# Weights in three tiles, another order of the projections, and where biases and key differences are computed, in an attention and expert kernel

## The chip, the cores and the metric

The kernel runs on one core of a Trainium2 chip. The metric is the device time of one execution in microseconds. Before the change three runs gave 4274.84, 4279.24 and 4280.67, median 4279.24. The profile is of another execution, which took 4282.12.

## The reference

The input x has 4 sequences of 2048 tokens with 512 features, in float32. It is normalized (layer norm), and two things are added to x: self-attention with 16 heads of 32 features, whose queries and keys pass a spectral filter, and a top-1 choice among 8 experts with 100 places each, which all share one weight.

```python
xn = _layernorm(x, axis=-1)
# attention
qkv = xn @ w_qkv
q, k, v = jnp.split(qkv, 3, axis=-1)          # then (B, H, S, dh)
mask = jax.nn.sigmoid(mask_logits)
q = _spectral_filter(q, mask)                 # rfft over dh, times mask, irfft
k = _spectral_filter(k, mask)
scores = jnp.einsum('bhqd,bhkd->bhqk', q, k) / math.sqrt(dh)
attn = jax.nn.softmax(scores, axis=-1)
out = jnp.einsum('bhqk,bhkd->bhqd', attn, v)
out = out.transpose(0, 2, 1, 3).reshape(B, S, D) @ w_out + b_out
# experts: each token's best one, the first 100 tokens of each
expert_out = dispatched @ w_expert + b_expert
combined = combine.reshape(-1, E * C) @ expert_out
x = x + out + combined
```

## The kernel before, in words

**Groups, blocks, halves.** The work is cut into 16 groups k: batch b = k // 4 and four heads c = k % 4. A group has four blocks n of 512 queries, a block 16 halves, one for each tile j of 128 keys, so a group has 64 halves (`GH`) and a block 16 (`HB`). Two halves, an even and an odd j, form a window. The whole main loop (lines 1013 to 1066) has 1024 halves. Every tensor is float32.

**What a half does.** For the heads in two pairs u: TensorE computes two products for the row maxima of a later block (`max_matmuls`, lines 497 to 507), 20 halves ahead of their use, and the two score tiles of this block (`scores`). The scores have keys in the partitions and go to banks 0 to 3 of the array. They are not computed from keys but from `steps_of_keys`, the difference of a key tile from the tile before it (`key_steps`, line 442), and added to what the bank holds; a block starts by writing the negated maxima there (`shift`). ScalarE takes exponentials of both (128x1024 each), VectorE reduces the products of the maxima (`max_reduce`, line 509), and TensorE multiplies the probabilities of the half before with the values (`products`, line 670), whose sum VectorE forms in `num`. Then come the half's planned steps, from `agenda`.

**Banks.** Banks 4 to 7 rotate (`turns`) among the maxima (two a pair), the products (one) and every planned step that uses TensorE (one). A maximum is one reduction for two neighbouring banks where u is 0 in the stream and the two are neighbours; else two.

**Row sums.** The row sums are formed by adding all probability tiles of a block: an accumulating DMA that GpSimd issues adds the odd tile to the even one (`pair`, 1 MB), and GpSimd adds the even tile of the window before (`add_to`), two instructions of 128x1024.

**Maxima of a block.** When all maxima of a block exist, VectorE takes the negated maximum (`max_negate`), TensorE transposes it at the next even half (`max_close`, line 527), ScalarE copies it to `row` and `rest`, GpSimd splits it at the start of the next window into three bfloat16 parts (`max_split`), and SP's queue moves the three rows to `negm`, which `shift` reads at the start of the block.

**Planned steps.** `plan` (line 907) lays into the halves of group k what the group k + 1 needs. Each of its 48 pieces (`projections`, line 469) is 16 matmuls over one tile of 128 tokens, for a query, a key or a value. `spread` (line 846) walks through the pieces in their order and finds the lowest level at which all fit before the half `last`; each half's `costs` count what is planned there already. Keys may come only after the old keys are spent (`after_keys_are_spent`, the bound `SPENT`), and the key differences come at 54, 58, 62 and 66 halves after the group's start. The list of groups `CROWDED` has another order. The weights of a group are one tile `wg` of three parts (query, key, value) with one buffer, loaded again (`load_qkv_weights`, line 414) after the last piece that reads it.

**Closing a block.** `close_steps` (line 689): row sums to `den` at half 5 of the next block, eight reciprocals on VectorE at halves 6 to 13, the division on GpSimd, four output projections at halves 17 to 20 (`result`, line 707: TensorE, then ScalarE copies the bank into `y`), then an accumulating DMA from `y` to the output.

**The token stage.** In the third group of a batch (c = 2) the next batch is loaded tile by tile (`load_tile`), measured on VectorE (`bn_stats`, `bn_aggr`), given the attention's output bias on GpSimd (`bias`, line 251) and written to the output (`first_sums`, line 255), onto which the later DMAs accumulate. In the fourth group the tiles are loaded again, normalized on ScalarE and turned on TensorE (`turn`) into `xnT`. For the first batch the load, the bias and the write stand in group 0.

**What sets the order.** Each engine runs its instructions in the order of the program (`InOrder`); SP's queue issues its DMAs in the same way. Line 84 is the helper that records every operation, so the profile's groups are told apart by tiles.

Of the kernel before, what the change touches and what calls it, by code (L numbers as in the profile page):

```python
# [25 lines left out]
P = 128  # L26
# [77 lines left out]
def attention_and_top1_experts(ctx: ExitStack, tc: tile.TileContext, a: dict, out: bass.AP):  # L104
# [90 lines left out]
    def filter_steps(c):  # L195
# [13 lines left out]
        def filtered(s):  # L209
# [6 lines left out]
            if c == 0:  # L216
                on.scalar.copy(wg[0][:, :, s, :], done)
            else:
                on.scalar.copy(wt[:, 1, :], pw)
                nc.sync.dma_start(out=wd[c][:, :, s, :], in_=wt[:, 1, :].rearrange("p (r n) -> p r n", r=NR))  # L220
# [9 lines left out]
    def token_stage(b):  # L230
# [20 lines left out]
        def bias(i):  # L251
            row = held[i // TQ][:, i % TQ, :]
            on.gpsimd.tensor_tensor(row, row, b_out, ALU.add)

        def first_sums(i):

            n, t = divmod(i, TQ)
            on.sync.dma_start(out=o[b, n, :, t : t + 1, :], in_=held[n][:, t : t + 1, :])
# [149 lines left out]
        return load, measure, scale, normalize, turn, route, bias, first_sums, load_tile  # L408
# [5 lines left out]
    def load_qkv_weights(k):  # L414
        wg[k] = weights.tile([P, NR, 3, P], F32, name="wg", bufs=1)
        on.sync.dma_start(out=wg[k], in_=wd[k % NG])
# [12 lines left out]
    def query_key(k, n, s, first, last):  # L429
# [3 lines left out]
        for r in range(NR):  # L433
            columns(pq, wg[k][:, r, s, :], xnT[:, r, cols], start=(r == 0), stop=(r == NR - 1))
# [7 lines left out]
    def key_steps(n):  # L442

        here = slice(n * QB, (n + 1) * QB)
        on.gpsimd.tensor_tensor(
# [6 lines left out]
    def value(k, n, first, last):  # L452
# [3 lines left out]
        for t in range(first, last):  # L456
            i = n * TQ + t
            for r in range(NR):
# [3 lines left out]
                    wg[k][:, r, 2, :],  # L462
# [6 lines left out]
    def projections(k, tiles=1):  # L469
# [5 lines left out]
        else:  # L475
            late = [(value, n) for n in range(2, NQ)] + [(query_key, 1, 0)]
            order = [(query_key, 0, 0)] + [(value, n) for n in range(2)] + (late if k not in CROWDED else [])
            order += [(query_key, n, 1) for n in range(NQ)] + (late[::-1] if k in CROWDED else [])
            order += [(query_key, n, 0) for n in range(2, NQ)]
# [29 lines left out]
    def max_reduce(item, half):  # L509
# [3 lines left out]
        whole = joined(*half) if u == 0 else joined(*half, apart=True)  # L513
        for heads, products_of in whole:
# [37 lines left out]
    def expert_steps():  # L552


        def begin():
            w_exp = chunk("w_exp")
            on.sync.dma_start(out=w_exp, in_=a["L0_ffn_w_expert"].rearrange("(r p) n -> p r n", p=P))
            b_exp = b_out
# [130 lines left out]
    def close_steps(k, n):  # L689
# [17 lines left out]
        def result(t):  # L707
            if t == 0:
                held["y"] = chunk("y")
            on.scalar.copy(held["y"][:, t, :], project(k, held["ot"], t))  # L710
# [29 lines left out]
    load, measure, scale, normalize, turn, first_route, first_bias, first_sums, load_tile = token_stage(0)  # L740
# [5 lines left out]
    wg[0] = weights.tile([P, NR, 3, P], F32, name="wg", bufs=1)  # L746
    nc.sync.dma_start(out=wg[0][:, :, 2, :], in_=w_qkv[:, :, 2 * DM : 2 * DM + P])
# [12 lines left out]
    nc.sync.dma_start(out=wd[0], in_=wg[0])  # L760
# [51 lines left out]
    for i, item in enumerate(stream[:MAX_AHEAD]):  # L812
# [6 lines left out]
        max_reduce(item, half)  # L819
# [83 lines left out]
    def keys_from(k):  # L903

        return (9 if k in CROWDED else 6) * TQ

    def plan(k):
# [4 lines left out]
        def after_keys_are_spent(steps, start):  # L912

            first = len(steps) - keys_from(k + 1)
            for i in range(NT):
                cost, _, step = steps[first + i]
                steps[first + i] = cost, start + SPENT + i // TQ * TQ, step

        if k == 0:
            for i in range(NT):  # L920
                half = 2 + i + 5 * (i // TQ)
                at(half, load_tile, i)
                at(half + 4, first_bias, i)
                at(half + 6, first_sums, i)
# [3 lines left out]
        last = start + GH - 4  # L928
        steps = []
        if k == 0:  # L930
            done = spread([(1, 0, step) for step in first_projections], 15)
            at(done[-1] + 1, load_qkv_weights, 1)
            plan_route(20, lambda i: first_route[i]())
            ready = done[-1] + 3
        if c == NG - 2 and b + 1 < B:

            at(start + 20, begin_stage, b + 1)
            for i in range(NT):
                half = start + 20 + i + 5 * (i // TQ)
                at(half, in_stage, 8, i)  # L940
                at(half + 3, in_stage, 1, i)
                at(half + 4, in_stage, 6, i)
                at(half + 6, in_stage, 7, i)
# [162 lines left out]
```

## Time and profile before

| what | us |
|---|---|
| median of three runs | 4279.24 |
| the profiled execution | 4282.12 |
| its span | 4280.0 |
| VectorE: maxima, 2576 of 128x512 | 1633.2 (683 ns each) |
| VectorE: maxima, 760 of 128x1024 | 925.0 (1217 ns each) |
| VectorE: sums of products, 960 | 650.3 (677 ns each) |
| VectorE: reciprocals, 504 | 274.3 (545 ns each) |
| GpSimd: additions for the row sums, 876 | 2121.5 |
| GpSimd: output bias on x, 64 | 92.5 |
| GpSimd: key differences, 64 | 87.7 |
| ScalarE: copies to y, 252 | 147.5 (586 ns each) |
| from issue to landing: even<-odd, 1 MB, median | 8.2 |
| from issue to landing: out_dram<-y, 1 MB, median | 10.1 |

The span is the time between the first and the last instruction of the profiled execution. A row of groups shows busy time, number and mean of one instruction; where a row merges shapes, the table above has them apart. A timeline row has its start, its length, the engine, the operation, the tiles written and read, and in brackets the idle time before it with what ended it. TensorE's float32 matmuls appear twice each, and the ends of matmuls are modelled, so starts are compared. VectorE's instructions overlap by some 0.08 us: 683 ns long, but 598 from start to start. The main loop's first half starts at 100.4 us, and four undisturbed groups take 252.2 us each.

### The profile page before, as it was taken

Reading aid. Unit: us, or ns where it says so; the run is one execution under the profiler, and the core shown is the slowest. Engines: PE = TensorE matmul, PEld = TensorE weight load, DVE = VectorE, ACT = ScalarE, POOL = GpSimd, SP = SyncE. Lnnn points to the kernel's source line nnn. Section 1 sums busy time; section 2 is a strip of 40 time slices with the busy share of each in tenths; the row PEclk is TensorE's granted clock in tenths of the full one; section 3 lists DMA queues with packets and bytes.
Section 4 is the critical chain, followed back from the end, with each engine's and each line's share of the span. In section 5 each row is a group of like instructions: output and inputs, shape, how many; then the busy total and the mean of one; then the engine's idle time right before and its main releaser. Section 6 shows DMA issues by size and latency. Waiting matters only on the chain.

```text
span 4280.0 us, 120579 instructions
## 1 busy us (share of the span) xinstructions
PE 4194.3 (98%) x52270; PEld 1854.3 (43%) x52270; DVE 3411.0 (80%) x5102; ACT 2525.3 (59%) x3475; POOL 3037.6 (71%) x2110
## 2 busy tenths in 40 slices
PE   8999999999999999999999999999999999999998
PEld 4444444434444444443444444443444444444432
DVE  6767888877788888887778888887778887788885
ACT  2556655666566556557556666555755565556665
POOL 1678777876776767777677766778668776676773
PEclk9999999999999999999999999999999999999999
DMA  4767778887687778888677787888877886778788
GB/s 109 179 149 152 153 160 173 191 201 151 137 159 153 156 152 165 182 195 186 132 158 151 158 159 146 170 188 194 170 140 152 175 164 131 148 162 161 154 168 167
DMA packets 163452, 690.16 MB, mean 161 GB/s; under 512 B 27414, under 2 KB 32696, under 8 KB 97640
## 3 DMA queue, kind: packets, MB, share of 16 engines
q0 software_dynamic: 110432, 605.83, 72.1%
q1 hardware_dynamic: 51312, 76.10, 5.7%
q8 instruction: 409, 6.70, 0.6%
q14 instruction: 123, 1.01, 0.1%
q10 hardware_dynamic: 1176, 0.52, 0.1%
HBM read 59.27 MB, written 88.96 MB: 35 GB/s over the span
## 4 chain that ended last, share of the span: by engine, by line
PE 89%; DVE 6%; DMA 2%; POOL 2%; issue 1%; ACT 0%; ACTq 0%; POOLq 0%; DVEq 0%
PE array L84 89%; DVE part L84 4%; DMA even<-odd 2%; POOL even L84 1%; DVE num L84 0%; DVE stats L84 0%; DMA negm<-row 0%; DVE factor L84 0%; POOL xs L84 0%; DMA odd<-in_L_attn_w_qkv_dram 0%; DVE mv L84 0%; POOL row L84 0%; POOL rstd L84 0%; DVE even L84 0%; POOL rest L84 0%
## 5 line engine op out<-in xcount | busy, mean ns | idle before, releaser
L84 DVE TENSOR_REDUCE part<-array 128x1 f32<-128x512 f32 (+1 forms) x3336 | 2497.1, 805 | 761.6 <-PE array L84 758.3
L84 POOL TENSOR_TENSOR even<-even 128x1024 f32<-128x1024 f32 x876 | 2121.5, 2524 | 425.9 <-DMA even<-odd 417.8
L84 PE MATMUL array<-keys,q 32*128 32x512 f32 x8192 | 2089.7, 615 | 10.9 <-DVE part L84 5.5
L84 PE MATMUL array<-q,steps_of_keys 32*128 32x512 f32 x8192 | 2022.7, 618 | 3.3 <-ACT odd L84 1.7
L84 ACT ACTIVATE even<-array 128x1024 f32<-128x1024 f32 x1024 | 993.5, 1021 | 491.3 <-PE array L84 455.6
L84 ACT ACTIVATE odd<-array 128x1024 f32<-128x1024 f32 x1024 | 993.3, 1021 | 458.8 <-PE array L84 378.5
L84 PEld LDWEIGHTS array<-keys,q 32*128 32x128 f32 x8192 | 784.3, 185 | 591.3 <-DVE part L84 365.3
L84 PEld LDWEIGHTS array<-q,steps_of_keys 32*128 32x128 f32 x8192 | 707.2, 184 | 267.3 <-issue 233.1
L84 POOL DMA_DIRECT2D even<-odd x510 | 463.4, 909 | 402.2 <-ACT odd L84 321.4
L84 DVE TENSOR_TENSOR num<-num,array 128x512 f32<-128x512 f32 x960 | 650.3, 677 | 26.3 <-PE array L84 17.2
L84 PE MATMUL array<-odd,v 128*32 128x512 f32 x4096 | 549.4, 608 | 2.4 <-DVE part L84 2.4
L84 PE MATMUL array<-even,v 128*32 128x512 f32 x4096 | 547.4, 606 | 2.9 <-DVE part L84 2.9
L84 PEld LDWEIGHTS array<-xnT,wg 128*32 128x32 f32 x15808 | 439.0, 110 | 256.2 <-DVE part L84 176.2
L84 PE MATMUL array<-xnT,wg 128*32 128x128 f32 (+1 forms) x15808 | 522.0, 277 | 11.4 <-DVE part L84 10.6
L84 PEld LDWEIGHTS array<-wg,xnT 128*32 128x32 f32 x8192 | 227.9, 110 | 129.2 <-DVE part L84 94.4
L84 DVE RECIPROCAL factor<-den 128x64 f32<-128x64 f32 x504 | 274.3, 545 | 0.0
L84 PE MATMUL array<-wo,ot 128*32 128x512 f32 x2048 | 267.8, 596 | 4.0 <-POOL ot L84 4.0
L84 PE MATMUL array<-wg,xnT 128*32 128x128 f32 x8192 | 263.5, 273 | 4.4 <-DVE part L84 4.4
L84 PEld LDWEIGHTS array<-odd,v 128*32 128x32 f32 x4096 | 81.0, 108 | 394.1 <-DVE part L84 384.9
L84 PEld LDWEIGHTS array<-even,v 128*32 128x32 f32 x4096 | 80.8, 108 | 393.8 <-DVE part L84 382.7
L84 POOL DMA_DIRECT2D out_dram<-y x63 | 83.7, 1329 | 212.4 <-ACT y L84 190.9
L84 ACT COPY y<-array 128x512 f32<-128x512 f32 x252 | 147.5, 586 | 139.8 <-PE array L84 139.4
(129 smaller groups left out, 1490.5 us busy)
## 6 DMA issues: line engine op xcount, KB each, us to landing
even<-odd POOLq DMA_DIRECT2D x510, 1024.0 KB, 8.2
out_dram<-y POOLq DMA_DIRECT2D x63, 1024.0 KB, 10.1
xs<-in_L_attn_x_dram SPq DMA_DIRECT2D x112, 256.0 KB
out_dram<-xs SPq DMA_DIRECT2D x64, 256.0 KB
wg<-wd SPq DMA_DIRECT2D x15, 768.0 KB
wo<-in_L_attn_w_out_dram SPq DMA_DIRECT2D x16, 256.0 KB
negm<-row SPq DMA_DIRECT2D x192, 4.0 KB
xs<-in_L_attn_x_dram SPq DMA_DIRECT2D x2, 1024.0 KB
```

Source lines behind the costliest of these rows:

```text
L84: done = act(*args, **kwargs)
```

## The change

1. The weights of a group lie in three tiles (query, key, value), each with one buffer and its own reload after its own last piece. The reload reads a third of the stored weights.
2. The order of the pieces. A usual group projects all values first, then two blocks of queries, all keys, and the other queries; the first group of a batch starts with three blocks of values and has the last later, and a `CROWDED` one starts with two. Pieces may reach the half 63 of the group (60 before). A turned tile counts 0.5 in place of 1, the transposed maxima 0.25 in place of 0.5.
3. The transpose of the maxima (`max_close`) stands behind the half's planned steps, not ahead of them.
4. In a half without planned TensorE work the second pair's maxima are reduced apart; in the lead-in all pairs may be joined.
5. The output bias is no longer added to x. In the groups with c = 0 VectorE adds it to the output projection on the way to `y`; the others keep the copy on ScalarE. The first write of the output is one DMA per block of 512 tokens from x to the output, without SBUF. Group 0 loads no tiles for it.
6. The key differences are formed by VectorE.
7. The expert's bias has a tile of its own.

```diff
-    def load_qkv_weights(k):
-        wg[k] = weights.tile([P, NR, 3, P], F32, name="wg", bufs=1)
-        on.sync.dma_start(out=wg[k], in_=wd[k % NG])
+    def load_qkv_weights(k, s):
+        wg[k, s] = weights.tile([P, NR, P], F32, name=f"w{s}", bufs=1)
+        on.sync.dma_start(out=wg[k, s], in_=wd[k % NG][:, :, s, :])
...
-        def bias(i):
-            row = held[i // TQ][:, i % TQ, :]
-            on.gpsimd.tensor_tensor(row, row, b_out, ALU.add)
-
-        def first_sums(i):
-
-            n, t = divmod(i, TQ)
-            on.sync.dma_start(out=o[b, n, :, t : t + 1, :], in_=held[n][:, t : t + 1, :])
+        def first_sums(n):
+
+            on.sync.dma_start(out=o[b, n], in_=x[b, n])
...
     def key_steps(n):
...
-        on.gpsimd.tensor_tensor(
+        on.vector.tensor_tensor(
             steps_of_keys[:, here],
...
-            late = [(value, n) for n in range(2, NQ)] + [(query_key, 1, 0)]
-            order = [(query_key, 0, 0)] + [(value, n) for n in range(2)] + (late if k not in CROWDED else [])
-            order += [(query_key, n, 1) for n in range(NQ)] + (late[::-1] if k in CROWDED else [])
-            order += [(query_key, n, 0) for n in range(2, NQ)]
+            first = 2 if k in CROWDED else 3 if k % NG == 0 else 4
+            queries, vals = ([(f, n, *s) for n in range(NQ)] for f, *s in ((query_key, 0), (value,)))
+            news = [(query_key, n, 1) for n in range(NQ)]
+            if first == 4:
+                order = vals + queries[:2] + news + queries[2:]
+            else:
+                order = vals[:first] + queries[:1] + news[:3]
+                order += vals[first : first + 1] + news[3:] + vals[first + 1 :] + queries[1:]
+        kinds.extend((2 if f is value else at[1]) for f, *at in order for t in range(0, TQ, tiles))
...
-    def max_reduce(item, half):
+    def max_reduce(item, half, apart=True):
...
-        whole = joined(*half) if u == 0 else joined(*half, apart=True)
-        for heads, products_of in whole:
+        for heads, products_of in joined(*half, apart):
...
-            on.scalar.copy(held["y"][:, t, :], project(k, held["ot"], t))
+            if k % NG == 0:
+                on.vector.tensor_tensor(held["y"][:, t, :], project(k, held["ot"], t), b_out, ALU.add)
+            else:
+                on.scalar.copy(held["y"][:, t, :], project(k, held["ot"], t))
...
-            for i in range(NT):
-                half = 2 + i + 5 * (i // TQ)
-                at(half, load_tile, i)
-                at(half + 4, first_bias, i)
-                at(half + 6, first_sums, i)
+            for n in range(NQ):
+                at(2 + (TQ + 5) * n, first_sums, n)
...
-        last = start + GH - 4
+        last = start + GH - 1
...
-                at(half, in_stage, 8, i)
+                at(half, in_stage, 7, i)
                 at(half + 3, in_stage, 1, i)
-                at(half + 4, in_stage, 6, i)
-                at(half + 6, in_stage, 7, i)
...
+                at(start + 26 + (TQ + 5) * n, in_stage, 6, n)
...
-                    steps.append((1, start + late[i] if i in late else 0, lambda i=i: in_stage(4, i)))
+                    steps.append((0.5, start + late[i] if i in late else 0, lambda i=i: in_stage(4, i)))
...
         if k + 2 < B * NG:
-            at(done[-1] + 1, load_qkv_weights, k + 2)
+            for s in range(3):
+                at(places[s][-1] + 1, load_qkv_weights, k + 2, s)
...
-        costs[block * HB - 4] += 0.5
+        costs[block * HB - 4] += 0.25
...
-                            max_reduce(mate, mh)
+                            max_reduce(mate, mh, u == 0 or not costs[2 * window + (j == odd)])
...
+                    for step in agenda[2 * window + (j == odd)]:
+                        step()
                     if j == even and window in full:
                         splits[window + 1] = full.pop(window)
                         max_close(*splits[window + 1])
-                    for step in agenda[2 * window + (j == odd)]:
-                        step()
```

`places[s]` are the halves at which the pieces of kind s (0 query, 1 key, 2 value) were laid; `kinds` lists the kind of each step in the order in which they are spread.

## The prediction

> **What bounds the kernel now.** I read the page's busy times and chain of waits first, then TensorE's timeline half by half, then VectorE's and GpSimd's timelines around the halves that are longer than their work.
>
> ```profile
> PE 4194.3 (98%) x52270; PEld 1854.3 (43%) x52270; DVE 3411.0 (80%) x5102; ACT 2525.3 (59%) x3475; POOL 3037.6 (71%) x2110
> ...
> PE 89%; DVE 6%; DMA 2%; POOL 2%; issue 1%; ACT 0%; ACTq 0%; POOLq 0%; DVEq 0%
> ```
>
> TensorE sets the end. How much of that is work shows in its timeline. A half (one key tile j) begins with its first scores matmul, array<-q,steps_of_keys; the distance between two such starts is the half's time.
>
> ```profile
> 1588.72 0.70 PE L84 MATMUL array<-q,steps_of_keys 32*128 32x512 f32 x2
> ...
> 1592.52 0.70 PE L84 MATMUL array<-q,steps_of_keys 32*128 32x512 f32 x2
> ...
> 1595.32 0.38 PE L84 MATMUL array<-square,neg 128*16 128x128 f32 x2
> 1596.14 1.08 PE L84 MATMUL array<-xnT,wg 128*32 128x128 f32 x32 [0.44 <-DVE part L84]
> ...
> 1597.16 0.70 PE L84 MATMUL array<-q,steps_of_keys 32*128 32x512 f32 x2
> ```
>
> The first half takes 3.80 us: scores, maxima, products and one added piece (a projection of 16 small matmuls). The second has a piece too and takes 4.64, since the transpose of the maxima stands ahead of the piece, takes the next bank, and the piece must wait for the joined maximum (the 0.44). I took this distance for all 1024 halves and counted the pieces in each. With one piece: 3.80 (3.78 behind an output projection or row sum). Two: 4.67. Three: 5.57. So a piece is 0.87, and work alone would make a bare half 3.80 - 0.87 = 2.93. Bare halves, though, take 3.35 to 3.63 in most places (3.55 taken), as VectorE's four maxima and one sum then set the pace. Every bare half wastes about 0.62.
>
> VectorE's margin in a half with one piece shows where other work comes ahead of its maxima.
>
> ```profile
> 1764.83 0.54 DVE L84 RECIPROCAL factor<-den 128x64 f32<-128x64 f32 x1
> 1765.29 0.63 DVE L84 BATCH_NORM_STATS2 stats<-xs 128x6 f32<-128x512 f32 x1
> 1765.96 0.18 DVE L84 BATCH_NORM_AGGREGATE mv<-stats 128x2 f32<-128x6 f32 x1
> 1766.06 2.39 DVE L84 TENSOR_REDUCE part<-array 128x1 f32<-128x512 f32 x3
> ```
>
> That half began at 1764.55. A first maximum normally starts 1.15 us into its half; here 1.51, and the half took 4.10. So a maximum that starts 0.36 late costs 0.31: past a tolerance of 0.06, lateness of the first maximum goes straight to TensorE.
>
> Last, the ends of the three groups that load and measure the next batch (k = 2, 6, 10). They take 260.8, 263.0 and 261.7 us where an undisturbed group takes 252.2.
>
> ```profile
> PEld L84 <- DMA negm<-row: 7.4, 1, 7.4
> ...
> 869.45 4.67 POOL L84 TENSOR_TENSOR even<-even 128x1024 f32<-128x1024 f32 x2 [5.36 <-DMA even<-odd]
> ...
> 889.36 0.42 POOL L84 TENSOR_TENSOR rest<-rest,row 16x128 f32<-16x128 f32 x1
> ```
>
> The next block's negated maxima are split on GpSimd at 889.4, though their half began at 883.1: GpSimd's queue is late with additions whose DMA was itself late, while the DMA share stands between 0.99 and 1.11 from 856 to 880 us.
>
> **The change part by part.** The sum is made against the profiled span, 4280.0 us.
>
> *Projections in every half.* Counted from the two programs' orders of instructions, bare halves fall from 137 to 90, halves with one piece rise from 673 to 764, with two fall from 201 to 162, with three from 10 to 3. One merge (a bare half and a double become two singles) saves 3.55 + 4.67 - 2 x 3.80 = 0.62; 47 of them give 29. Turned tiles count as pieces there but cost 0.58, which leaves 27. Bounds 15 and 33.
>
> *Transposed maxima behind the pieces.* 46 halves will hold one piece and then a transpose. 44 such halves now: 4.64 to 4.65 in 29, 4.28 to 4.29 in 12, the rest longer; mean about 4.55. Behind the piece the transpose no longer delays it (3.80 + 0.21 of its own, as the block starts show: 4.01 with their four small matmuls), but the next maxima need the bank that the products' sum frees 4.16 to 4.22 into the half, so I take 4.25: 46 x 0.30 = 14. Bounds 5 and 25. ScalarE's copies come 0.9 later; GpSimd reaches the split about 4.5 us after the transpose in an undisturbed group (620.3, 624.9), which hides it.
>
> *Maxima apart in bare halves.* A bare half with no reciprocal and its maxima apart can release the bank sooner (3.09 us for the half that begins at 1659.6, its four maxima apart, against 3.63 joined); 14 such halves x 0.5 = 7, less 2 for those with a reciprocal, where two reductions (2 x 0.598 from start to start) replace one of 1.131: 5. Bounds 0 and 12.
>
> *Bias and copies x to out by DMA alone.* GpSimd loses 64 bias additions (92.5 us) and the 64 key differences (87.7). The stores no longer wait for GpSimd's bias; the 768 KB weight load at 872.4, in the middle of the crowd, becomes three of 256 KB, two of them earlier. Both go against the lateness at the ends of k = 2, 6, 10. The stalls there are worth 6.6 + 1.5, 5.7 + 1.8 and 6.6 + 1.5 against the undisturbed 3.35 and 3.65: 24 in all. I take 20; bounds 0 and 27. The remaining excess is measuring on VectorE, which stays. The copies are 16 of 1 MB where 64 stores of 256 KB went, the same bytes; out_dram<-y, also 1 MB, takes 10.1 to land. Its waiters (the accumulating adds) come at least 10 halves later. Weights: no wait for wg appears in the trace, and each third now has more than 20 halves (76 us) from reload to use. Both at nothing. If that cover goes, TensorE waits up to 10 per group start.
>
> *Output bias on VectorE.* 64 sums of an array bank, about the 0.677 of num<-num,array. VectorE is idle 0.77 before the maxima, so its time is hidden, but the bank is freed at 0.37 + 0.68 = 1.05 into the next half, where the second maxima want it at 0.96: 64 x 0.1 = 6. Bounds 0 and 13.
>
> *Key differences on VectorE.* Four per group, 15 groups (four more in the prologue, where about 1.3 of joined reductions pays for them: 0). Queued behind each are the maxima, and TensorE waits for those. Alone it takes about 0.6 (64 POOL ones are 1.37). It can start 0.35 into its half, 0.81 where a reciprocal precedes it, as in two of the four. Without a wait: 0.35 + 0.6 = 0.95 is before 1.15 and free; 0.81 + 0.6 is 0.26 late, 0.2 lost. That is 15 x 2 x 0.2 = 6. But it reads two tiles in SBUF, as GpSimd does all the time.
>
> ```profile
> 30.31 0.16 DVE L84 SCALAR_TENSOR_TENSOR shift<-mv,rstd 128x4 f32<-128x4 f32 x1 [1.48 <-POOL rstd L84]
> ...
> 35.15 1.22 DVE L84 SCALAR_TENSOR_TENSOR shift<-mv,rstd 128x4 f32<-128x4 f32 x1 [1.47 <-POOL rstd L84]
> ```
>
> ```profile
> 35.09 1.26 POOL L84 TENSOR_TENSOR steps_of_keys<-keys 128x512 f32<-128x512 f32 x1
> ```
>
> The same tiny instruction with two SBUF inputs takes 0.16 alone and 1.22 when a GpSimd instruction started just before; it ends 0.02 after that one. GpSimd's additions last 2.36 each in steady state, in pairs; in 322 of 480 odd halves one is running 0.4 us in, where the key differences fall. A mean wait of half of 2.36 is 1.18. Without a reciprocal, 0.2 of it is free: 0.65 x 1.0 = 0.65 lost. With one: 0.65 x 1.4 + 0.35 x 0.2 = 0.97. Per group 2 x 0.65 + 2 x 0.97 = 3.2; 15 groups: 48. Bounds: 6 with no wait at all, 120 if each waits 2.0 to the end of a pair.
>
> The Trainium skill speaks against this part: "SBUF — State Buffer", section "Who interferes with whom", says that a VectorE instruction with two SBUF inputs contends with a GpSimd one that reads SBUF, and that the later one is blocked for the whole instruction. The row at 35.15 agrees. By the rule every overlap costs the rest of an addition, which is my 48; by the row of undisturbed VectorE adds the part would cost 6 and the sum would be 42 lower. The output bias has one input in the array, and by the same section does not contend.
>
> Sum: 4280 - 27 - 14 - 5 - 20 + 6 + 48 = 4268. The profiled execution took 4282.1, 2.9 over the median of the three runs; taken over as a difference of -12, the median 4279.2 becomes **4267**. Its own range, with the smaller bounds, is 4245 to 4288.
>
> **The rivals.** *The shared path decides (slower).* The key differences wait for both additions of a pair, 2.0 each on 60 places: 120 in place of 48 gives 4339. It turns the sign from 60 us on, 1.0 per difference. For it: the additions come back to back. Against: GpSimd has lost work, so may have finished sooner; two of three only.
>
> *The differences slip between.* GpSimd, lighter, finishes before the odd half's start, and only 6 is lost: 4225. For it: the free slots in the trace (at half 62 of several groups GpSimd had not begun). Against: additions wait for their DMAs, not for GpSimd.
>
> *The late ends stay (not faster).* The 1 MB copies go out in the same crowded stretch, so the 20 does not come and a block start or two per batch is late by 7: 4268 + 20 + 10, near 4297. For it: the DMA share of 1.1. Against: stores no longer wait there.
>
> **How the numbers follow.** Forecast 0.45, first rival 0.20, second 0.22, third 0.13. The time is 4267. The range takes in the second rival and most of the way to the first: 4222 to 4312. A measurement of this kernel tells 0.2% (8.6 us) from no change. Faster: 0.6 of the forecast and the second rival, 0.49. Same: 0.35 of the forecast and half of the third, 0.22. Slower: the rest, 0.29.
>
> **What would show it.** Bare halves should be 90 and the undisturbed groups about 249 before the differences' loss. Halves with transposes near 4.25. TensorE's wait for negm at 880 to 900 should be gone. The key differences on VectorE would show as 0.6 alone and up to 2.4 beside GpSimd, with halves 55, 59, 63 and 3 of each group longer. All of them near 0.6, or many over 3, and the forecast is wrong.

## The result, and the profile after

| | before | changed |
|---|---|---|
| median of runs, us | 4279.95 | 4334.92 |
| lowest to highest, us | 4274.84 to 4280.74 | 4323.62 to 4336.31 |
| profiled execution, us | 4282.12 | 4336.31 |
| its span, us | 4280.0 | 4334.5 |

The changed kernel is slower: its time over that of before is 1.0125 (95% interval 1.0106 to 1.0144). The forecast was 4267, the first rival's time 4339. A *span* below is that of a profiled execution; a *ratio* sets the times of a kernel against those of the kernel before, run beside it. The page of the changed kernel, busy times and the first line of the chain of waits:

```profile
PE 4198.4 (97%) x52270; PEld 1874.3 (43%) x52270; DVE 3579.5 (83%) x5263; ACT 2492.6 (58%) x3411; POOL 2895.8 (67%) x1982
...
PE 85%; DVE 12%; issue 2%; DMA 1%; POOL 0%; ACT 0%; ACTq 0%; POOLq 0%; DVEq 0%
```

VectorE's busy time is up by 168 us and its share of the chain has doubled, from 6% to 12%, while GpSimd's fell from 2% to nothing. Among the costliest groups of instructions, the line of the products of maxima and values carries the new idle time: in its last field, what TensorE sat idle ahead of them. Before it was 2.9 us.

```profile
L84 PE MATMUL array<-even,v 128*32 128x512 f32 x4096 | 553.2, 612 | 90.7 <-DVE part L84 90.6
```

These are the odd halves' products, and they wait for VectorE's maxima. The moved key differences fall in odd halves. The view of their tile on VectorE gives the shortest, median and longest duration in ns:

```profile
L84 DVE TENSOR_TENSOR steps_of_keys<-keys x64: 625/1776/5661, 40.0 to 4101.8; 128x512 f32<-128x512 f32 x64
```

Alone the instruction takes 0.63 to 0.68 us. The 60 behind the prologue sum to 139, so some 98 of it is waiting, 1.6 each on the mean. One of them with its surroundings, from the timelines of VectorE, GpSimd and TensorE at the end of group 4 (start, duration, instruction, and in brackets the idle time ahead):

```profile
1423.99 0.68 DVE L84 TENSOR_TENSOR num<-num,array 128x512 f32<-128x512 f32 x1
1424.59 3.89 DVE L84 TENSOR_TENSOR steps_of_keys<-keys 128x512 f32<-128x512 f32 x1
1428.40 2.47 DVE L84 TENSOR_REDUCE part<-array 128x1 f32<-128x512 f32 x4
```

```profile
1422.92 5.00 POOL L84 TENSOR_TENSOR even<-even 128x1024 f32<-128x1024 f32 x2
1430.77 0.88 POOL L84 DMA_DIRECT2D even<-odd  x1 [2.86 <-PE array L84]
```

```profile
1424.25 0.70 PE L84 MATMUL array<-q,steps_of_keys 32*128 32x512 f32 x2
...
1429.13 1.06 PE L84 MATMUL array<-even,v 128*32 128x512 f32 x8 [2.90 <-DVE part L84]
...
1430.36 1.09 PE L84 MATMUL array<-q,steps_of_keys 32*128 32x512 f32 x2
```

GpSimd's two additions run back to back from 1422.92 to 1427.92. The key difference is issued at 1424.59, while the *first* of them is running, and ends at 1428.48: 0.56 after the *second*. It was not let in between the two. Its half has begun at 1424.25; the first maximum, which belongs at 1.15 into the half, starts at 4.15, and TensorE stands 2.90. The half takes 6.11 in place of some 3.3. The next half, from 1430.36 to 1435.82, pays too: the granted clock of TensorE is 0.69 of full speed in it, against 1.00 in the same half of experiment 1. The last of TensorE's rows above shows it, 1.09 in place of 0.70. That half takes 5.46 where 3.92 is taken there.

Of the 60 differences, 56 met an addition, and each ended 0.55 or 0.56 us after the end of one. 37 came during the last addition of a run, or the only one, and waited for it alone (they last 1.75 on the mean). 16 came during the first of two and waited for both, as above (4.25). But 3 came during the first and ended between the two. One of these, from the timelines of VectorE and GpSimd in group 2:

```profile
852.75 1.09 DVE L84 TENSOR_TENSOR steps_of_keys<-keys 128x512 f32<-128x512 f32 x1
```

```profile
853.26 2.81 POOL L84 TENSOR_TENSOR even<-even 128x1024 f32<-128x1024 f32 x1
```

The first addition of this pair runs from 850.93 to 853.29. The difference ends at 853.84, 0.55 after it, while the second addition is already running, and that one takes 2.81 where some 2.4 to 2.7 is usual. The profile shows what tells the two kinds apart, the seam between the additions: here the second begins 0.03 before the first ends, and in the 16 that waited for both it begins 0.32 to 0.38 before (at 1425.26 in the pair above, whose first ends at 1425.62).

Of the forecast's signs of being wrong, one came: 19 of the 60 differences take over 3 us. The signs of its other parts came as written. Bare halves are 90 by the program's order; most halves with a transpose of the maxima and one piece take 4.22 to 4.28; and between 800 and 905 us TensorE no longer waits for negm.

### The profile page after: what moved, and what is told of

Same layout as the page of the kernel before. It is cut to its first block, busy times and chain, and to the rows that moved or that the text cites. A ratio compares the mean times of both kernels' runs of the same rounds, so it can differ in the third digit from the quotient of the medians.

```text
span 4334.5 us, 120459 instructions
## 1 busy us (share of the span) xinstructions
PE 4198.4 (97%) x52270; PEld 1874.3 (43%) x52270; DVE 3579.5 (83%) x5263; ACT 2492.6 (58%) x3411; POOL 2895.8 (67%) x1982
## 4 chain that ended last, share of the span: by engine, by line
PE 85%; DVE 12%; issue 2%; DMA 1%; POOL 0%; ACT 0%; ACTq 0%; POOLq 0%; DVEq 0%
PE array L84 85%; DVE part L84 7%; DVE steps_of_keys L84 2%; DVE num L84 1%; DVE stats L84 1%; DVE factor L84 1%; DMA even<-odd 1%; DVE mv L84 0%; POOL even L84 0%; DMA odd<-in_L_attn_w_qkv_dram 0%; POOL rstd L84 0%; ACT odd L84 0%; DVE y L84 0%; DMA mask<-_L_attn_mask_logits_dram 0%; DVE xs L84 0%
## 5 line engine op out<-in xcount | busy, mean ns | idle before, releaser
L84 PE MATMUL array<-q,steps_of_keys 32*128 32x512 f32 x8192 | 2048.4, 621 | 4.2 <-issue 2.2
L84 POOL DMA_DIRECT2D even<-odd x510 | 451.1, 885 | 652.5 <-ACT odd L84 431.5
L84 PE MATMUL array<-even,v 128*32 128x512 f32 x4096 | 553.2, 612 | 90.7 <-DVE part L84 90.6
L84 PEld LDWEIGHTS array<-xnT,w 128*32 128x32 f32 x15808 | 449.3, 111 | 263.3 <-DVE part L84 166.7
L84 PE MATMUL array<-xnT,w 128*32 128x128 f32 (+1 forms) x15808 | 528.0, 279 | 0.8 <-ACT xnT L84 0.7
L84 PEld LDWEIGHTS array<-w,xnT 128*32 128x32 f32 x8192 | 230.1, 110 | 146.1 <-DVE part L84 101.9
L84 PE MATMUL array<-w,xnT 128*32 128x128 f32 x8192 | 268.5, 273 | 1.3 <-DVE num L84 1.2
L84 ACT COPY q<-array 128x128 f32<-128x128 f32 (+1 forms) x250 | 67.2, 269 | 231.9 <-PE array L84 225.8
```

Source lines behind the costliest of these rows:

```text
L84: done = act(*args, **kwargs)
```

## The experiments

**1. Key differences back on GpSimd, all else as changed.**

```diff
     def key_steps(n):
-        on.vector.tensor_tensor(
+        on.gpsimd.tensor_tensor(
```

> The changed kernel with the key differences back on GpSimd, nothing else. Theory (VectorE's difference is blocked by GpSimd's pair of additions, about 8 us per group in the halves 55, 59, 63, 0 and 3): 15 groups x 8 = 120 come back, 4215 us, between 4205 and 4235. Rival (the new order of the pieces or the copies from x to the output cost the time, and the differences only sit where it shows): no more than 40 come back, 4295 or above.

Measured: 4225.44 (4224.29 to 4229.49), ratio to before 0.9869 [0.9853, 0.9886], span 4222.5. So one instruction's engine is worth 112 us in spans, and the rest of the change gains 57.5. Most of the 112 is idle time of TensorE ahead of the odd halves' products, 90.7 against 4.0 here. Another part is the clock that the stalls leave behind: its mean grant is 0.989 in the changed kernel and 0.996 here, and 0.7% of the span is some 30 (the two parts overlap). The page of this kernel, the same two lines:

```profile
PE 4174.2 (99%) x52270; PEld 1866.4 (44%) x52270; DVE 3451.7 (82%) x5199; ACT 2490.6 (59%) x3411; POOL 2960.3 (70%) x2046
...
PE 93%; DVE 4%; DMA 2%; issue 0%; POOL 0%; ACT 0%; SPq 0%; ACTq 0%; POOLq 0%; DVEq 0%
```

The end of group 4 again, VectorE's and GpSimd's timelines; its half 63 runs from 1397.17 to 1400.47:

```profile
1396.91 0.68 DVE L84 TENSOR_TENSOR num<-num,array 128x512 f32<-128x512 f32 x1
1398.31 2.48 DVE L84 TENSOR_REDUCE part<-array 128x1 f32<-128x512 f32 x4 [0.72 <-PE array L84]
```

```profile
1395.84 5.00 POOL L84 TENSOR_TENSOR even<-even 128x1024 f32<-128x1024 f32 x2
1400.48 1.58 POOL L84 TENSOR_TENSOR steps_of_keys<-keys 128x512 f32<-128x512 f32 x1
```

The pair of additions lies across the half's start just as it did above, but VectorE now sits idle 0.72 for TensorE, the first maximum starts 1.14 into the half, and the half takes 3.30. The key difference stands behind the additions in GpSimd's own queue, where nothing urgent waits.

What seven of the 16 groups of 64 halves took (us, by the first scores of each):

| group | before | changed | exp. 1 | changed less exp. 1 |
|---|---|---|---|---|
| 1 | 251.7 | 255.0 | 249.5 | 5.5 |
| 2 | 260.8 | 263.8 | 251.9 | 11.9 |
| 4 | 252.2 | 255.2 | 250.6 | 4.6 |
| 5 | 252.2 | 257.6 | 249.8 | 7.8 |
| 6 | 263.0 | 264.6 | 252.0 | 12.6 |
| 8 | 252.1 | 255.4 | 250.0 | 5.4 |
| 10 | 261.7 | 265.4 | 251.9 | 13.5 |

The places are far from equal. Summed over the 15 groups, the halves 63 cost 43 us more than in experiment 1 and the halves behind them 12, the halves 59 cost 36, and the halves 55 and 3 cost 10 each.

In groups 2, 6 and 10, which load the next batch, the additions' own DMAs are late and a whole pair of additions stands ahead of the key difference. The timelines of VectorE, GpSimd and TensorE in group 2 of the changed kernel:

```profile
869.39 5.57 DVE L84 TENSOR_TENSOR steps_of_keys<-keys 128x512 f32<-128x512 f32 x1
```

```profile
869.48 4.91 POOL L84 TENSOR_TENSOR even<-even 128x1024 f32<-128x1024 f32 x2
```

```profile
875.61 1.93 PE L84 MATMUL array<-even,v 128*32 128x512 f32 x8 [4.98 <-DVE part L84]
```

The additions end at 874.39, the difference at 874.96, and TensorE stands 4.98. Then it goes on at half its clock (0.51 from 874 to 881), and the half takes 10.55 in place of 3.80. By the profile's starts this difference was issued 0.09 ahead of the first addition, while GpSimd was issuing a DMA (868.81 to 869.73), and was held all the same.

**2. Key differences on VectorE, all else as before.** The opposite edit, on the kernel before.

> The kernel before with the key differences on VectorE, nothing else. Theory: the wait comes from GpSimd's additions, which are there in both kernels, so 60 to 130 us are lost here too: 4340 to 4410. Rival (only the fuller group ends of the changed kernel make the differences costly): under 30 lost, below 4310.

Measured: 4350.19 (4348.35 to 4355.6), ratio 1.0162 [1.0145, 1.0178], span 4346.5: 66.5 lost in spans. The view of the tile:

```profile
L84 DVE TENSOR_TENSOR steps_of_keys<-keys x64: 627/1372/4664, 40.3 to 4116.6; 128x512 f32<-128x512 f32 x64
```

The move loses on either kernel. It costs less here, where a difference takes 1.69 on the mean (108.2 / 64) against 2.2 in the changed kernel: 42 of the 60 met an addition, against 56, and 8 waited for both of a pair, against 16.

**3. The same instruction on VectorE with one operand in an array bank.** ScalarE copies the keys into a bank first.

```diff
     def key_steps(n):
+        copy = bank()
+        on.scalar.copy(copy, keys[:, here])
         on.vector.tensor_tensor(
             steps_of_keys[:, here],
             keys[:, P + here.start : P + here.stop],
-            keys[:, here],
+            copy,
             ALU.subtract,
```

> The changed kernel, differences on VectorE, but ScalarE first copies the older keys into an array bank, so that VectorE reads one tile from SBUF and one from the array. Theory (the two SBUF inputs are what makes it wait): each difference takes 0.68 us with no wait, and the time is about 4225, the sum of the first experiment plus up to 12 for the longer VectorE queue. Rival (VectorE is simply full at the group's end): 0.6 us more of VectorE work costs the same as before, 4300 or above.

Measured: 4273.44 (4269.51 to 4278.52), ratio 0.9979 [0.9969, 0.9989], span 4271.4.

```profile
L84 DVE TENSOR_TENSOR steps_of_keys<-keys,array x64: 655/687/690, 40.9 to 4039.5; 128x512 f32<-128x512 f32 x64
```

The cause of the wait is shown: with one input out of SBUF none of the 64 waits at all, though 53 of the 60 behind the prologue run beside an addition. The total is a miss all the same, 48 above experiment 1. The halves in which the copy takes its bank mostly take 4.22 to 4.29, where 3.80 is usual for one piece, and cost 23 more in sum than in experiment 1; the halves behind them, in which VectorE forms the difference, cost 26. The wait went, and the copy with its bank took its place; which of these two costs the time no run shows.

**4. Each key difference one half later,** so in even halves.

```diff
         for n in range(NQ):
-            at(start + GH - 10 + n * TQ, key_steps, n)
+            at(start + GH - 9 + n * TQ, key_steps, n)
```

> The changed kernel with each key difference planned one half later, so that it stands at the start of an even half. Theory: the wait depends on where in GpSimd's window the difference falls. An addition runs at 0.4 us into 245 of 479 even halves against 322 of 480 odd ones, so about a third to a half of the 120 comes back: 4270 to 4300. Rival (the number of VectorE instructions counts, not their place): unchanged, 4325 to 4345.

Measured: 4283.32 (4271.79 to 4290.39), ratio 0.9997 [0.9986, 1.0008], span 4279.6.

```profile
L84 DVE TENSOR_TENSOR steps_of_keys<-keys x64: 626/684/6139, 39.8 to 4052.3; 128x512 f32<-128x512 f32 x64
```

The median is that of an undisturbed instruction, and half of the loss is back. Three of the four places of a group are nearly free (means of 0.68 to 0.82), where GpSimd has mostly finished its pair. The fourth, in half 60, still takes 2.73 on the mean and up to 6.14, with halves of 4.6 to 11.4. What VectorE pays hangs on where GpSimd's additions lie, not on the instruction.

**5. GpSimd's additions cut in two:** four of 512 columns in a run in place of two of 1024.

```diff
         for u in range(2):
-            engine.tensor_tensor(tile[:, u], tile[:, u], sum_before[:, u], ALU.add)
+            for h in range(2):
+                engine.tensor_tensor(tile[:, u, h], tile[:, u, h], sum_before[:, u, h], ALU.add)
```

> The changed kernel (key differences on VectorE) with each of GpSimd's row-sum additions cut into two of 512 columns, four in a run in place of two. Theory A (a waiting difference is let through only when GpSimd's run of additions is over): the waits stay, 4320 to 4350. Theory B, the prediction's (it waits for the running instruction alone): the mean wait halves and some 40 to 60 us come back, 4270 to 4295.

Measured: 4340.35 (4339.32 to 4354.96), ratio 1.0155 [1.0136, 1.0174], span 4337.5. The view of the tile, then one difference from VectorE's timeline and the run of additions from GpSimd's:

```profile
L84 DVE TENSOR_TENSOR steps_of_keys<-keys x64: 629/1640/7502, 39.2 to 4104.9; 128x512 f32<-128x512 f32 x64
```

```profile
1432.27 4.14 DVE L84 TENSOR_TENSOR steps_of_keys<-keys 128x512 f32<-128x512 f32 x1
```

```profile
1430.60 5.25 POOL L84 TENSOR_TENSOR even<-even 128x512 f32<-128x512 f32 x4
```

If VectorE waited for one GpSimd instruction at a time, halving it would halve the wait. It did not: the 64 sum to 139.8 against 141.6. Here the difference comes 1.67 into a run of four and ends at 1436.41, again 0.56 after the last of the four (1435.85).

Not every seam holds, though. In this run 40 seams between two additions held a difference and 9 let one in. Taken with the changed kernel and experiments 2 and 4, 69 seams held and 19 let in, and the profile parts them without an exception: the second addition begins 0.15 to 0.40 us before the first ends where it held, and 0.03 to 0.07 before where it let in. In 18 of the 19, GpSimd had begun the run after standing idle; in all 69 others the run followed at once on its instruction before. So the wait goes on to the end of the additions that overlap, and can end between two that barely do.

**6. The output bias taken off VectorE** (on experiment 1; the attention's output bias is left out).

```diff
-            if k % NG == 0:
-                on.vector.tensor_tensor(held["y"][:, t, :], project(k, held["ot"], t), b_out, ALU.add)
-            else:
-                on.scalar.copy(held["y"][:, t, :], project(k, held["ot"], t))
+            on.scalar.copy(held["y"][:, t, :], project(k, held["ot"], t))
```

> The first experiment's kernel (key differences on GpSimd) with every output projection copied by ScalarE; this leaves the attention's output bias out. Theory of the prediction: the bias on VectorE costs 6 us, so 4219. Rival: the undisturbed c = 0 groups are only 0.5 us longer than their neighbours in that run, so 2 us at most, 4223 to 4226.

Measured: 4217.59 (4215.8 to 4218.63), ratio 0.9858 [0.9841, 0.9874], span 4216.3. The bias on VectorE costs 6.2 in spans, 4.7 by the ratios. It reads the array and one tile in SBUF, and shows no wait (0.675 to 0.692 each in the changed kernel).

**7. The transposed maxima ahead of the planned steps again** (on experiment 1).

```diff
-                    for step in agenda[2 * window + (j == odd)]:
-                        step()
                     if j == even and window in full:
                         splits[window + 1] = full.pop(window)
                         max_close(*splits[window + 1])
+                    for step in agenda[2 * window + (j == odd)]:
+                        step()
```

> The first experiment's kernel with the transpose of the maxima ahead of the half's pieces again. Theory: 46 halves lose about 0.30 each, +14 us, 4236 to 4243. Rival (another wait takes its place and the gain was nothing): 4223 to 4228.

Measured: 4234.93 (4234.0 to 4238.6), ratio 0.9898 [0.9882, 0.9915], span 4236.8: 14.3 lost in spans, 12.4 by the ratios.

**8. The transposed maxima behind the steps, on the kernel before.** The opposite edit.

> The kernel before with the transpose of the maxima behind the half's pieces, nothing else. Theory: 44 halves from 4.59 to 4.24, 15 us, 4260 to 4270. Rival (ScalarE's later copies make GpSimd's split and the next block's start late): 4278 or above.

Measured: 4264.34 (4258.58 to 4266.5), ratio 0.9966 [0.9955, 0.9978], span 4262.1: 14.5 gained by the ratio and 17.9 in spans. The 44 halves with a transpose and one piece went from 4.58 to 4.28, which is 13.2. TensorE's timeline in one such half of experiment 1, from one half's scores to the next's:

```profile
1196.17 0.70 PE L84 MATMUL array<-q,steps_of_keys 32*128 32x512 f32 x2
...
1198.97 1.06 PE L84 MATMUL array<-w,xnT 128*32 128x128 f32 x32
1199.84 0.38 PE L84 MATMUL array<-square,neg 128*16 128x128 f32 x2
...
1200.46 0.70 PE L84 MATMUL array<-q,steps_of_keys 32*128 32x512 f32 x2
```

The piece runs on without the 0.44 of waiting that the prediction showed, then the transpose: 4.29.

**9. The old bounds of the spread** (on experiment 1): the pieces end three halves earlier, turned tiles count 1 and transposes 0.5 again.

```diff
-        last = start + GH - 1
+        last = start + GH - 4
...
-                    steps.append((0.5, start + late[i] if i in late else 0, lambda i=i: in_stage(4, i)))
+                    steps.append((1, start + late[i] if i in late else 0, lambda i=i: in_stage(4, i)))
...
-            steps[0] = (0.5, first, steps[0][2])
+            steps[0] = (1, first, steps[0][2])
...
-        costs[block * HB - 4] += 0.25
+        costs[block * HB - 4] += 0.5
```

> The first experiment's kernel with the planner's bounds of before (last half 60, a turned tile counts 1, the transposed maxima 0.5); the order of values, queries and keys stays new. Its halves have 138 bare, 672 with one piece and 199 with two, as before. Theory: 27 us are lost, 4247 to 4257. Rival (bare halves are no slower than their share, the order of the pieces brought the gain): 4223 to 4232.

Measured: 4232.04 (4230.55 to 4236.26), ratio 0.9896 [0.9879, 0.9912], span 4228.7: 6 lost in spans, 12 by the ratios, though it has 138 bare halves. The 27 of the theory did not come; the time is at the upper end of the rival's range. TensorE's timeline, the starts of halves 61, 62 and 63 of group 5, the first two bare:

```profile
1641.72 0.70 PE L84 MATMUL array<-q,steps_of_keys 32*128 32x512 f32 x2
...
1644.82 0.70 PE L84 MATMUL array<-q,steps_of_keys 32*128 32x512 f32 x2
...
1648.21 0.70 PE L84 MATMUL array<-q,steps_of_keys 32*128 32x512 f32 x2
```

These two bare halves take 3.10 and 3.39, each with a reciprocal on VectorE, not the 3.55 that I took from before.

**10. Maxima of bare halves apart, alone on the kernel before.**

```diff
-        whole = joined(*half) if u == 0 else joined(*half, apart=True)
+        whole = joined(*half, apart or u == 1)
...
-                            max_reduce(mate, mh)
+                            max_reduce(mate, mh, not costs[2 * window + (j == odd)])
```

> The kernel before with the maxima apart in halves without planned work, nothing else. Theory (bare halves took 3.65 because of the joined maximum; in the last run with as many bare halves they took 3.17): some 70 to 100 bare halves gain 0.3 to 0.5, 4235 to 4260. Rival (the prediction's, a gain in the few without a reciprocal): 4268 to 4275.

Measured: 4270.65 (4265.54 to 4276.86), ratio 0.9983 [0.9974, 0.9993], span 4271.2: 7 to 9 gained. The 135 bare halves that the trace shows went from 3.66 to 3.55 on the mean, 14.7 in sum, and the halves with pieces lost 5.5 of it. The larger gain that I expected by then did not come.

**11. One reload of all three weights, behind the group's last piece** (on experiment 1).

```diff
             for s in range(3):
-                at(places[s][-1] + 1, load_qkv_weights, k + 2, s)
+                at(done[-1] + 1, load_qkv_weights, k + 2, s)
```

> The first experiment's kernel, still three weight tiles, but all three reloaded after the last piece of the group. Theory (the three tiles are what allows values at the first half and pieces up to the last): the first value piece of the next group waits for a reload that has only begun, 4 to 8 us in each of 14 groups, 4280 to 4340. Rival (the reload is hidden anyway): 4223 to 4230.

Measured: 4283.51 (4281.19 to 4288.26), ratio 1.0013 [1.0004, 1.0023], span 4285.8. TensorE's timeline at the start of group 5, and the wait in the view of waits (total, times, longest):

```profile
1421.58 1.07 PE L84 MATMUL array<-odd,v 128*32 128x512 f32 x8
1426.64 1.93 PE L84 MATMUL array<-w,xnT 128*32 128x128 f32 x32 [4.00 <-DMA w<-wd]
```

```profile
PE array L84 <- DMA w<-wd: 46.9, 12, 7.2
```

The first piece of a group comes in its first half now, and the pieces reach the group before's last half: a reload behind them is late at once, 63 us in spans. The prediction put the three tiles at nothing with 10 per group start if the cover goes; twelve waits of 3.9 on the mean, and 63 / 15 = 4.2 a group, is what its going costs. The waits are 47 of the 63; the mean granted clock, 0.990 against 0.996 in experiment 1, fell with them.

**12. The token stage as before** (on experiment 1): tiles loaded for group 0, bias on GpSimd, 64 stores of 256 KB, copies of the projection on ScalarE.

```diff
-        def first_sums(n):
+        def bias(i):
+            row = held[i // TQ][:, i % TQ, :]
+            on.gpsimd.tensor_tensor(row, row, b_out, ALU.add)
+
+        def first_sums(i):
 
-            on.sync.dma_start(out=o[b, n], in_=x[b, n])
+            n, t = divmod(i, TQ)
+            on.sync.dma_start(out=o[b, n, :, t : t + 1, :], in_=held[n][:, t : t + 1, :])
...
+                at(half + 4, in_stage, 8, i)
+                at(half + 6, in_stage, 6, i)
...
-                at(start + 26 + (TQ + 5) * n, in_stage, 6, n)
```

> The first experiment's kernel (key differences on GpSimd) with the output bias added to x by GpSimd, stores tile by tile after it, and the loads of group 0, all as before; output projections copied by ScalarE. Theory (GpSimd's lateness at the ends of groups 2, 6 and 10 came from this): those groups go back from 252 to 258 to 262, and the time from 4225 to 4240 to 4250. Rival (the lateness came from the 768 KB reload of weights in the same stretch): the groups stay at 252 to 254, the time at 4220 to 4228.

Measured: 4250.9 (4244.81 to 4251.77), ratio 0.9935 [0.9919, 0.9952], span 4243.0. Set against experiment 6, which has the same copies of the projection, it is 26.7 in spans and 33 by the ratios. Groups 2, 6 and 10 take 259.8, 260.8 and 261.6 (252 in experiment 6), and their half 63 some 9.8 in place of 3.3. At the end of group 2, whose half 62 begins at 868.20, GpSimd's timeline and TensorE's wait:

```profile
873.80 4.65 POOL L84 TENSOR_TENSOR even<-even 128x1024 f32<-128x1024 f32 x2 [1.66 <-DMA even<-odd]
878.42 0.42 POOL L84 TENSOR_TENSOR rest<-rest,row 16x128 f32<-16x128 f32 x1
```

```profile
PE array L84 <- DMA negm<-row: 6.8, 1, 6.8
```

The same place in experiment 1, where half 62 begins at 872.57:

```profile
869.93 4.67 POOL L84 TENSOR_TENSOR even<-even 128x1024 f32<-128x1024 f32 x2 [0.89 <-DMA even<-odd]
874.57 0.42 POOL L84 TENSOR_TENSOR rest<-rest,row 16x128 f32<-16x128 f32 x1
```

The split of the maxima comes 2.0 into half 62 there and 10.2 here: GpSimd's late queue was the stall, and the new token stage takes it away. Which part of it does, the additions of the bias that GpSimd no longer makes or the stores, no run shows, since they went back together.

## Why the prediction was wrong

The mechanism was named and the size was off. Term by term, in us against the span of before:

| term | forecast (bounds) | measured | by |
|---|---|---|---|
| key differences on VectorE | +48 (6 to 120) | +112 | exp. 1 |
| projections in every half | -27 (15 to 33) | -6 to -12 | exp. 9 |
| transposed maxima behind | -14 (5 to 25) | -12 to -18 | exps. 7, 8 |
| maxima apart | -5 (0 to 12) | -7 to -9 on before | exp. 10 |
| token stage and copies | -20 (0 to 27) | -27 to -33 | exp. 12 |
| bias on VectorE | +6 (0 to 13) | +5 to +6 | exp. 6 |
| all but the key differences | -60 | -57.5 | exp. 1 |

**The step that failed** is the size of the wait: the sentence "A mean wait of half of 2.36 is 1.18", with the 0.65 of the places in which an addition runs. Together they are 0.77 of waiting a place; measured are 1.6. TensorE was to lose 48 / 60 = 0.8 at each, and lost 112 / 60 = 1.9. The runs show three things in place of that step.

- *More places met an addition*, 56 of 60 (0.93). The 0.65 was counted in the kernel before, and with the differences on VectorE there (experiment 2) it was 42 of 60. The rest of the change moves the additions against the halves: at 0.4 us into these 60 halves an addition runs in 39 of them before and in 48 of experiment 1.
- *The wait can go on through the second addition.* It did in 16 places, which adds 37 us to the waits there. The step let a difference wait for the one addition that it meets.
- *A stall costs TensorE more than its length*, by the clock that is granted behind it (0.989 against 0.996 over the span). The prediction has no term for that.

The first rival named the second of these, at a price of 2.0 for each difference: 4339 against 4334.9. That its time is so near is luck in part, since 16 of the 60 waited for both additions and the other two causes made up the rest. It was given 0.20, and the evidence for it stood in the same text ("the additions come back to back"). The row I rested the size on, at 35.15 us, showed one GpSimd instruction with nothing behind it, so it could not tell one from a run.

The rule of the Trainium skill ("SBUF — State Buffer", section "Who interferes with whom") agrees in kind with experiment 3, in which the wait went with the second SBUF input. It speaks of one instruction that blocks another; here the block went on through two additions in 16 of 60 places, 3.89 us in the row above, and through four in experiment 5. The measurement decides.

**The projections** were the second wrong size. I priced the merge of a bare half with a double at 3.55 + 4.67 - 2 x 3.80 = 0.62 by the bare halves of before. But other parts of the same change make bare halves cheaper: those of experiment 9 that the new bounds fill take 3.32 on the mean. With that, 3.32 + 4.67 - 7.60 = 0.39 a merge, and 47 of them give 18. Two parts took some of the same waste, and I added them. That is still more than the 6 to 12 measured, and what takes the rest stays open.

**The token stage** was forecast too small, since I left "the remaining excess" of groups 2, 6 and 10 to the measuring on VectorE. In experiment 1 these groups take 252, some 2 over their neighbours, with the measuring still there; before they took 9 to 11 over. The transposes, the bias and the maxima apart came near their terms, and the three weight tiles cost nothing to speak of (TensorE waited 1.2 in all for their reloads in experiment 1). That the errors of these terms cancelled (-60 against -57.5) is luck in part.

**The third rival** is refuted by experiment 12's comparison: the late ends went. In the changed kernel they are hidden, since groups 2, 6 and 10 lose 12 to 13.5 to the key differences instead.

The best version with the whole result is that of experiment 1, the change without its sixth part: 4225.44 us, 1.3% faster than before and 2.5% faster than the changed kernel.

## What to carry to other kernels

Before an instruction with two SBUF inputs moves to VectorE, look at what GpSimd runs back to back at that moment, and price the wait to the end of the run, not to the end of one instruction; then ask who is queued behind the waiting instruction, and count where the places fall in the kernel as it will be, not as it was. If the place is bad, leave the instruction behind GpSimd's own work or move it to where GpSimd is idle; an operand in an array bank removed the wait here, but the copy and its bank cost 48. Price each part of a change with the other parts in place, since two of them may remove the same idle time.

## What was not expected of the hardware

A VectorE instruction that met GpSimd additions ended 0.55 or 0.56 us after the end of one, in all of 56 cases. Where the next addition had begun 0.15 us or more before that end, VectorE did not get in between (69 seams of four runs), although each addition is an instruction of its own; where it had begun 0.07 or less before, VectorE did (19 seams), and the addition took longer in its turn. That is what the times show; by what means VectorE is kept out stays open, as no run sets the overlap by itself. The longest wait, in experiment 5, made 7.50 us of an instruction that takes 0.63, beside a division, a DMA issue and four additions in a row on GpSimd. The same instruction with one operand in an array bank took 0.655 to 0.690 in all of 64 cases.

Behind a stall TensorE was often granted half its clock for 3.4 or 6.8 us. Between 110 and 4110 us the changed kernel has 16 such stretches, each of which begins 2 to 5 us after the start of a stall of 2.0 to 5.1 us; six stalls of 1.9 to 2.9 us had none. Experiment 1 has one stretch there.
